# Eight groups of a graph layer's indirect row gathers put in other forms

## The chip, the cores and the metric

The kernel runs on one core of a Trainium2 chip. The metric is the device time of one execution in microseconds. The core has five engines with instruction streams of their own: PE (matrix multiply; its weight loads are shown apart as PEld), DVE and ACT (elementwise work), POOL and SP. SP, ACT and POOL can also issue DMA transfers; the gathers that this document is about, transfers whose source rows are named by a list of indices, are issued by POOL.

## The reference, cut to what matters

A graph layer over N = 12500 nodes with 256 values each and E = 200000 edges, sorted by their target node:

```python
h = jnp.maximum(_layernorm(x, axis=-1), 0.0)
agg = jax.ops.segment_sum(h[src], dst, num_segments=N)
z = (1.0 + eps_gin) * h + agg
t = jnp.dot(z, W1) + b1                       # 256 -> 512
t = jax.nn.relu(_batchnorm(t, g1, bt1))
conv_out = jnp.dot(t, W2) + b2                # 512 -> 256
out = x + jax.nn.relu(_batchnorm(conv_out + h, g2, bt2))
```

`h[src]` takes one row of 256 float32 values (1 KB) for every edge. All values of `src` lie between 0 and 12499.

## The kernel before, in words

The edges are cut into 1563 tiles of 128 (the last has 64), and the tiles into 131 groups of GT = 12 (line 19; the last group has 3). For each tile one indirect DMA on POOL (line 517) brings the 128 rows of its edges into SBUF, one row to a partition; its indices are a column of `srcT`, which holds all source numbers with the edge of a tile on the partition axis. The first LEAD = 30 groups (line 22) gather from `x` and normalise the rows afterwards (`settle`, line 376); the others gather from the DRAM table `h_tab`, into which the kernel has by then written the normalised rows (`h_chunk`, line 476).

The order is written out by hand (`manual_schedule`, line 367). The main loop (line 642) runs over the groups. In step i it calls `gather(i + AHEAD)` with AHEAD = 4 (line 21), then the additions, copies and comparisons that belong to earlier groups, and then `sums(i)` (line 556), in which PE multiplies the group's gathered rows by 12 selection matrices `oh` and adds them up in one PSUM tile (line 570). Between these products it places the sum of group i - 2 (`put`, line 583), turns chunks of h, and does a slice of the first dense product (`slice_of`, line 601). When the groups are done, the first batch norm is closed, and the second product (line 800), the second batch norm and the output follow; POOL has no part in that.

`gather(i)` (lines 509 to 521) chooses where the rows land by i % 5: remainders 0 and 1 use the fixed tiles gta0/gtb0 and gta1/gtb1 (8 and 4 rows to a partition, lines 123 to 127), the others a tile `gt` of a pool with three buffers. It goes through the group's tiles backwards. Tiles that `alone(i)` (line 462) names are left out: in every ninth group from 40 to 121 (40, 49, 58, ...) tile 0 is fetched row by row by SP and tile 1 by ACT (class `Fetcher`, line 398). These single rows are read as bytes, through views of both sides that are cast to U8, with an address that a register holds (lines 444 to 447).

Two lines of the gather:

```python
out=slot(ga, t - t0)[:rows], out_offset=None, in_=x if i < LEAD else h_tab,
in_offset=bass.IndirectOffsetOnAxis(ap=srcT[:rows, t : t + 1], axis=0),
```

Both sides are float32, and no bound is given.

Of the kernel before, what the change touches and what calls it, by code (L numbers as in the profile page):

```python
# [8 lines left out]
I32 = mybir.dt.int32  # L9
U8 = mybir.dt.uint8  # L10
# [7 lines left out]
EPS = 1e-5  # L18
GT = 12
MARGIN = 64  # L20
AHEAD = 4
LEAD = 30
EARLY = 2
# [17 lines left out]
def kernel(  # L41
# [17 lines left out]
    N, D = x.shape  # L59
# [9 lines left out]
    for g in range(NCH):  # L69
        rows = min(CH, N - g * CH)  # L70
# [11 lines left out]
    STEP = -(-N * P * GT // E)  # L82
    WIDE = P + 2 * MARGIN
    NBLK = -(-max(NTILE, NG * GT) // P)
# [4 lines left out]
    h_tab = dram.tile([N, D], F32, name="h_tab")  # L89
# [25 lines left out]
    srcT = consts.tile([P, NBLK * P], I32, name="srcT")  # L115
# [13 lines left out]
    def slots(ga, t, n=1):  # L129

        for lo, hi, tile_ in ga:
            if lo <= t < hi:
                assert t + n <= hi
                return tile_[:, t - lo : t - lo + n, :]

    def slot(ga, t):
        return slots(ga, t)[:, 0, :]
# [26 lines left out]
    with ExitStack() as es:  # L164
# [54 lines left out]
        place = raw.tile([P, NG], I32, name="place")  # L219
        nc.gpsimd.iota(place, pattern=[[STEP, NG]], base=-MARGIN, channel_multiplier=0)  # L220
        nc.gpsimd.iota(col_i, pattern=[[1, WIDE]], base=0, channel_multiplier=0)
        nc.gpsimd.iota(row_i, pattern=[[0, 1]], base=0, channel_multiplier=1)
        for i in range(EARLY):
            for t in reversed(range(GT)):
                nc.gpsimd.indirect_dma_start(
                    out=slot(early[i], t), out_offset=None, in_=x,
                    in_offset=bass.IndirectOffsetOnAxis(ap=srcE[:, i * GT + t : i * GT + t + 1], axis=0),
# [10 lines left out]
        ends = raw.tile([P, 2], F32, name="ends")  # L238
        for k, end in enumerate((P, 2 * MARGIN + 1)):
            nc.vector.memset(ends[:, k : k + 1], float(1 - end))  # L240
# [79 lines left out]
    def fast():  # L320
# [24 lines left out]
        with ExitStack() as fs:  # L345
# [8 lines left out]
            with ExitStack() as es:  # L354
                ln = es.enter_context(tc.tile_pool(name="ln", bufs=2))
                gat = es.enter_context(tc.tile_pool(name="gat", bufs=AHEAD + 1 - EARLY))
                sel = es.enter_context(tc.tile_pool(name="sel", bufs=2))
# [100 lines left out]
                sp, act = mybir.EngineType.SP, mybir.EngineType.Activation  # L458
                hf = Fetcher(nc.sync, sp, h_tab, SP_PACE, LEAD - AHEAD + 1, NG - 1, (0,), "s")
                af = Fetcher(nc.scalar, act, h_tab, ACT_PACE, LEAD - AHEAD + 1, NG - CLOSE, (1,), "a")  # L460

                def alone(i):
                    return {f.slots[0]: f for f in (hf, af) if i in f.groups}
# [3 lines left out]
                def x_chunk(g):  # L467
                    if g >= NCH:
                        return
                    n = chunks[g][1] * R  # L470
                    xts[g] = ln.tile([P, R, D], F32, name="xt", bufs=4)
                    if n < CH:
                        nc.vector.memset(xts[g], 0.0)
                    carry(nc.sync, xts[g], x, g, store=False)
# [34 lines left out]
                def gather(i):  # L509
                    t0, n = groups[i]  # L510
                    k = i % (AHEAD + 1)
                    ga = early[k] if k < EARLY else ((0, GT, gat.tile([P, GT, D], F32, name="gt")),)
                    for t in reversed(range(t0, t0 + n)):
                        if t - t0 in alone(i):
                            continue
                        rows = left if t == full_tiles else P
                        nc.gpsimd.indirect_dma_start(  # L517
                            out=slot(ga, t - t0)[:rows], out_offset=None, in_=x if i < LEAD else h_tab,
                            in_offset=bass.IndirectOffsetOnAxis(ap=srcT[:rows, t : t + 1], axis=0),
                        )  # L520
                    gathered[i] = ga

                def span(i):
                    return STEP * i - MARGIN, STEP * i - MARGIN + WIDE

# [96 lines left out]
                def first(c):  # L622

                    return min(i for i in range(NG) if c in reach(i))
# [4 lines left out]
                for g in range(3):  # L629
                    x_chunk(g)  # L630
                for i in range(EARLY, min(AHEAD, NG)):
                    gather(i)
# [3 lines left out]
                for c in range(NCH):  # L636
                    k = min(max(first(c) + 1, c + 2), NG - CLOSE - 1)
                    loads.setdefault(k, []).append(c)
                    scales.setdefault(min(max(first(c) + 3, c + 3), NG - CLOSE), []).append(c)
                    assert c + 1 < k <= first(c) + 4 and c < LEAD - AHEAD  # L640
                added = whole = 0
                for i in range(NG - CLOSE):
                    before = added
                    gather(i + AHEAD)
                    for k, f in enumerate((hf, af)):
                        if i == hf.begin - 8 + k:
# [53 lines left out]
                for i in range(NG - CLOSE, NG + 1):  # L700
                    if i + AHEAD < NG:
                        gather(i + AHEAD)
                    hf.step(i)
                    if i < NG:
                        spots(i)
                    if i + 1 < NG:
                        edges(i + 1)
                    for c in scales.get(i, ()):
                        z_scale(c)
                    while near < i:  # L710
                        hold(near)
                        while added < near - 1:
                            add(added)
                            added += 1
                        put(near)
                        near += 1
                    while added < near:
                        add(added)
                        added += 1
                    while whole < NCH and last(whole) < added:  # L720
                        queue += [(whole, f) for f in range(HC)]
                        whole += 1
                    for c, f in queue:
                        slice_of(c, f)
                        take(c, f)
                    queue = []
                    if i < NG:
                        sums(i)
# [363 lines left out]
```

## Time and profile before

| | us |
|---|---|
| median of 3 runs | 2174.43 |
| lowest and highest | 2173.98 and 2178.93 |
| the profiled execution's own time | 2174.26 |
| its span, first to last instruction | 2172.5 |
| POOL busy | 1463.4 (67%) |
| PE busy | 1604.0 (74%) |
| DVE busy | 802.1 (37%) |
| ACT busy | 408.9 (19%) |

The profile shows one execution. Its page has the busy time of each engine, a strip of the span in 40 slices (a digit is the busy share in tenths), the DMA queues, the chain of work that ended last, and the costliest groups of instructions: the line and the engine, what is written from what, how often, the busy time and the mean length in ns, the idle time of the engine just before, and what ended most of it. "issue" there means that the engine waited for nothing that the profile shows. Busy time on POOL counts the instructions that it works on and not the pieces between them. Other views give one line's instructions with their shortest, median and longest durations, an engine's instructions in order of time, and the busy time of all engines in a stretch.

In the chain that ended last POOL's lines have 33%, DMA 20%, PE 20% and issue 17%.

### The profile page before, as it was taken

To read this page: it belongs to the slowest core of one execution; us is meant where nothing else is said; L and a number is where in the kernel's file an instruction comes from. 1 tells how busy PE (TensorE), PEld (TensorE's weight loads), DVE (VectorE), ACT (ScalarE), POOL (GpSimd) and SP (SyncE) were. 2 spreads that over 40 slices of the span, in tenths; PEclk is the share of its full clock that TensorE was granted. 3 is DMA by queue.
4 is the path that set the end of the run, shared out by engine and by line. 5 is a ranking of instruction groups with operands and counts; after the bars stand their busy time and mean duration, and the time that the engine had idled before them with its cause. 6 is when DMAs were issued, how large, how long until landed. Compare 5 with 4: busy or idle time off the path is not lost.

```text
span 2172.5 us, 20945 instructions
## 1 busy us (share of the span) xinstructions
PE 1604.0 (74%) x4874; PEld 982.7 (45%) x4874; DVE 802.1 (37%) x1285; ACT 408.9 (19%) x772; POOL 1463.4 (67%) x1555
## 2 busy tenths in 40 slices
PE   4576667777777776777777777767777777779996
PEld 3454545554444444434444444434444444444445
DVE  5655657652323223223223222322322322323336
ACT  4666667520000000000000000000000000014446
POOL 7777777777777777777777777777777777750000
PEclk9877989888888889889888987888888888989998
DMA  6676777554444444444444444444444444547967
GB/s 197 211 228 215 252 234 233 171 148 123 131 128 136 116 128 135 123 123 134 122 130 129 120 129 130 135 117 127 137 121 121 136 119 123 154 129 269 307 232 286
DMA packets 153844, 349.86 MB, mean 161 GB/s; under 512 B 33564, under 2 KB 63916, under 8 KB 153710
## 3 DMA queue, kind: packets, MB, share of 16 engines
q0 software_dynamic: 74048, 202.28, 33.4%
q1 hardware_dynamic: 42534, 83.96, 11.7%
q10 hardware_dynamic: 37128, 62.19, 8.3%
q8 instruction: 41, 0.67, 0.1%
q14 instruction: 93, 0.76, 0.1%
HBM read 284.29 MB, written 64.00 MB: 160 GB/s over the span
## 4 chain that ended last, share of the span: by engine, by line
POOL 33%; DMA 20%; PE 20%; issue 17%; ACT 6%; DVE 3%; POOLq 0%; ACTq 0%; DVEq 0%
POOL gt L517 29%; PE ps L570 8%; PE py L800 8%; DMA gta<-h_tab,srcT 6%; DMA gtb<-h_tab,srcT 6%; DMA gt<-h_tab,srcT 5%; POOL gta L517 3%; DMA gt<-in_x_dram,srcT 2%; PE ph L606 2%; ACT gt L394 2%; PE pz L588 2%; ACT yT L825 2%; DVE stg L383 1%; ACT gta L394 1%; DMA gta<-in_x_dram,srcT 1%
## 5 line engine op out<-in xcount | busy, mean ns | idle before, releaser
L517 POOL DMA_INDIRECT gt<-h_tab,srcT x708 | 670.2, 947 | 215.8 <-issue 208.2
L570 PE MATMUL ps<-gt,oh 128*128 128x256 f32 x1848 | 613.0, 456 | 243.0 <-DMA gt<-h_tab,srcT 220.3
L570 PEld LDWEIGHTS ps<-gt,oh 128*128 128x128 f32 x1848 | 367.8, 220 | 488.7 <-DMA gt<-h_tab,srcT 337.3
L617 DVE BATCH_NORM_STATS2 st<-ph 128x6 f32<-128x512 f32 (+1 forms) x100 | 68.4, 684 | 949.6 <-PE ph L606 949.6
L517 POOL DMA_INDIRECT gta<-h_tab,srcT x315 | 297.8, 946 | 96.1 <-issue 42.1
L570 PE MATMUL ps<-gta,oh 128*128 128x256 f32 x822 | 264.0, 439 | 72.4 <-DMA gta<-h_tab,srcT 71.3
L619 ACT COPY ts<-ph 128x512 f32<-128x512 f32 (+1 forms) x26 | 14.1, 544 | 1434.8 <-DVE st L617 1434.8
L588 PE MATMUL pz<-at,zs 128*128 128x256 f32 x524 | 205.6, 534 | 87.1 <-ACT zs L577 78.5
L517 POOL DMA_INDIRECT gt<-in_x_dram,srcT x216 | 204.3, 946 | 65.8 <-issue 60.9
L570 PEld LDWEIGHTS ps<-gta,oh 128*128 128x128 f32 x822 | 158.9, 213 | 180.0 <-DMA gta<-h_tab,srcT 145.4
L570 PE MATMUL ps<-gtb,oh 128*128 128x256 f32 x416 | 158.9, 499 | 95.2 <-DMA gtb<-h_tab,srcT 69.6
L549 DVE TENSOR_TENSOR oh<-col,dstT 128x1536 f32<-128x1536 f32 x131 | 228.1, 1741 | 0.0
L606 PE MATMUL ph<-zc,w1s 128*128 128x512 f32 (+1 forms) x400 | 203.4, 637 | 29.7 <-DVE hc L503 28.6
L588 PEld LDWEIGHTS pz<-at,zs 128*128 128x128 f32 x524 | 141.4, 276 | 131.4 <-ACT zs L577 97.6
L517 POOL DMA_INDIRECT gtb<-h_tab,srcT x160 | 151.4, 946 | 48.7 <-PE ps L570 27.1
L800 PE MATMUL py<-ti,w2s 128*128 128x512 f32 (+1 forms) x400 | 170.8, 590 | 3.7 <-ACT ti L787 3.7
L570 PEld LDWEIGHTS ps<-gtb,oh 128*128 128x128 f32 x416 | 89.9, 239 | 147.6 <-DMA gtb<-h_tab,srcT 73.8
L599 DVE TENSOR_TENSOR zc<-pz,zc 128x512 f32<-128x512 f32 (+8 forms) x187 | 93.0, 522 | 121.5 <-PE pz L588 91.5
L606 PEld LDWEIGHTS ph<-zc,w1s 128*128 128x128 f32 x400 | 80.4, 205 | 95.9 <-issue 52.7
L800 PEld LDWEIGHTS py<-ti,w2s 128*128 128x128 f32 x400 | 76.9, 193 | 97.7 <-issue 90.1
L394 ACT ACTIVATE gt<-gt,nbg,rsg 128x256 f32<-128x256 f32 x216 | 108.1, 586 | 9.1 <-DVE nbg L392 7.6
L787 ACT ACTIVATE ti<-ti,of,sc 128x512 f32<-128x512 f32 (+1 forms) x100 | 76.4, 798 | 89.3 <-DMA ti<-t_tab 74.0
(111 smaller groups left out, 978.9 us busy)
## 6 DMA issues: line engine op xcount, KB each, us to landing
t_tab<-ts ACTq DMA_DIRECT2D x96, 256.0 KB
ti<-t_tab SPq DMA_DIRECT2D x96, 256.0 KB
one_s<-h_tab SPq DMA_DIRECT2D x1280, 1.0 KB
one_a<-h_tab ACTq DMA_DIRECT2D x1280, 1.0 KB
xt<-in_x_dram SPq DMA_DIRECT2D x24, 512.0 KB
h_tab<-ht ACTq DMA_DIRECT2D x24, 512.0 KB
h_cols<-hc SPq DMA_DIRECT2D x24, 512.0 KB
zc<-h_cols SPq DMA_DIRECT2D x24, 512.0 KB
```

What stands on the lines that cost most here:

```text
L383: nc.vector.bn_stats(st[:, c : c + 2, :].rearrange("p c s -> p (c s)"), two.rearrange("p c d -> p d c"),)
L394: nc.scalar.activation(slot(to, c), slot(v, c), AF.Relu, bias=nb[:, c : c + 1], scale=rs[:, c : c + 1])
L517: nc.gpsimd.indirect_dma_start(out=slot(ga, t - t0)[:rows], out_offset=None, in_=x if i < LEAD else h_tab, in_offset=bass.IndirectOffsetOn ...
L549: nc.vector.tensor_tensor(ohs[i][:, :n, :], col[:, :P].unsqueeze(1).to_broadcast([P, n, P]), dstT[:, t0 : t0 + n].unsqueeze(2).to_broadcas ...
L570: nc.tensor.matmul(ps, lhsT=oh[:rows, j, :], rhs=fetched[:rows], start=(j == order[0]), stop=(j == order[-1]))
L588: nc.tensor.matmul(pz[:, d, :], lhsT=zs[:, d * P : (d + 1) * P], rhs=at, start=True, stop=True)
L599: nc.vector.tensor_add(side, pz[:, :, a - lo : b - lo], side)
L606: nc.tensor.matmul(ph[:, :n], lhsT=w1s[:, d, f * P : (f + 1) * P], rhs=zc[c][:, d, :n], start=(d == 0), stop=(d == DC - 1),)
L617: nc.vector.bn_stats(st1[:, f, c, :], ph[:, :n])
L787: nc.scalar.activation(tis[g, f][:, :n], tis[g, f][:, :n], AF.Relu, bias=of1[:, f : f + 1], scale=sc1[:, f : f + 1],)
L800: nc.tensor.matmul(pys[d][:, :n], lhsT=w2s[:, f, d * P : (d + 1) * P], rhs=tis[g, f][:, :n], start=(f == 0), stop=(f == HC - 1),)
L825: nc.scalar.activation(yT[g][:, d, :], yT[g][:, d, :], AF.Relu, bias=of2[:, d : d + 1], scale=sc2[:, d : d + 1])
```

## The change

A table names eight groups and a form for each two of them; every other group is gathered as before. Groups 40 and 41 get a bound of N - 1 = 12499 with errors off, so that a row whose index were above it would be left out; groups 50 and 51 the same bound with errors on, the default; groups 60 and 61 view the landing tile and the table as int32; groups 80 and 81 view both as bytes, so that a row is 1024 elements. The list of indices, the rows that are read, their places, the order and the number of the gathers stay.

```diff
+FORMS = {40: "skip", 41: "skip", 50: "stop", 51: "stop", 60: I32, 61: I32, 80: U8, 81: U8}
...
                         rows = left if t == full_tiles else P
+                        to, table, more = slot(ga, t - t0)[:rows], x if i < LEAD else h_tab, {}
+                        if i in FORMS:
+                            kind = FORMS[i]
+                            if kind == "skip":
+                                more = dict(bounds_check=N - 1, oob_is_err=False)
+                            elif kind == "stop":
+                                more = dict(bounds_check=N - 1)
+                            else:
+                                to, table = to.bitcast(kind), table.bitcast(kind)
                         nc.gpsimd.indirect_dma_start(
-                            out=slot(ga, t - t0)[:rows], out_offset=None, in_=x if i < LEAD else h_tab,
-                            in_offset=bass.IndirectOffsetOnAxis(ap=srcT[:rows, t : t + 1], axis=0),
+                            out=to, out_offset=None, in_=table,
+                            in_offset=bass.IndirectOffsetOnAxis(ap=srcT[:rows, t : t + 1], axis=0), **more,
                         )
```

## The prediction

> **What bounds the kernel.** I read the strip of 40 slices first, then the costliest groups, then POOL's lines in order of time, and last the packet counts by queue. From the page:
>
> ```profile
> span 2172.5 us, 20945 instructions
> PE   4576667777777776777777777767777777779996
> POOL 7777777777777777777777777777777777750000
> L517 POOL DMA_INDIRECT gt<-h_tab,srcT x708 | 670.2, 947 | 215.8 <-issue 208.2
> L517 POOL DMA_INDIRECT gta<-h_tab,srcT x315 | 297.8, 946 | 96.1 <-issue 42.1
> L517 POOL DMA_INDIRECT gtb<-h_tab,srcT x160 | 151.4, 946 | 48.7 <-PE ps L570 27.1
> ```
>
> POOL's strip is flat at 7 from the first slice to the 35th. That looks like an engine with a quarter of its time free; it isn't. The group rows say why: 215.8 us of idle over 708 gathers is 0.305 us ahead of each one, and most of it ends in "issue", which means that nothing the profile shows was waited for. So one gather occupies POOL for 0.946 + 0.305 = 1.251 us and the next follows at once. The table of busy time by stretch gives the steady state:
>
> ```profile
> 457.00:1936.60 1479.60, 1097.04 (x3152) 652.41 (x3152) 422.27 (x630) 13.89 (x28) 1119.31 (x1183) 0.86 0.46 129
> ```
>
> The columns are the length, then busy time and count for PE, PEld, DVE, ACT and POOL, then clock, DMA share and GB/s. 1183 gathers in 1479.6 us are 1.251 us apiece: POOL alone accounts for the whole stretch. PE is busy 74% of it and DVE 29%, and in the list of waits POOL's own waits for another engine are all 0.3 us long, the same as the idle piece that it has ahead of every gather. POOL is never late for want of a free slot. So a change of d us in one gather of this stretch moves everything behind it by d, to the end.
>
> Are the gathers of the change in this stretch? Group 40's first gather starts at 607 us and group 81's last at about 1224 us (counting gathers in order along POOL's line), so all are. Groups whose number leaves 0 or 1 modulo 5 are those that land in gta0/gtb0 and gta1/gtb1, so each form will be visible under these names. Group 40 has two of its twelve tiles fetched by SP and ACT, the other seven have all twelve on POOL: 22 gathers "skip", 24 "stop", 24 as 32-bit integers, 24 as bytes, 94 in all. I make the sum against the profiled execution: 2174.26 us, of which the span is 2172.5; the median of the three runs is 2174.43, 0.17 higher. About 0.3% of it, 6.5 us, is what a measurement of this kernel can tell from no change.
>
> **What a row of a gather costs.** The last group gives the one gather with half the rows (64 instead of 128), the second line here, in POOL's order of time (start, duration, and in brackets the idle before):
>
> ```profile
> 1931.94 0.95 POOL L517 DMA_INDIRECT gt<-h_tab,srcT  x1 [0.30 <-issue]
> 1933.19 0.90 POOL L517 DMA_INDIRECT gta<-h_tab,srcT  x1 [0.30 <-PE ps L570]
> 1934.40 0.96 POOL L517 DMA_INDIRECT gta<-h_tab,srcT  x1 [0.30 <-PE ps L570]
> ```
>
> It took 903 ns beside 946 (shortest and median of the line's view), so 64 rows are worth 43 ns, one row 0.67 ns, and all 128 rows 86 ns. Over nine tenths of a gather is independent of its rows. This single gather is all that the trace has on the matter, and the chance below is set accordingly.
>
> **Part 1: the bound, 46 gathers (22 + 24).** No gather of before has one, so the price is bounded. What is added is a comparison of 128 indices with 12499; no index exceeds it, so nothing is ever skipped or reported, and "skip" and "stop" have one answer. The nearest row is the 0.67 ns: if comparing a row costs as much as all that is done for a row now, a gather grows by 86 ns, and 46 x 0.086 = 4.0 us. From below: the row part can't fall by more than itself, -4.0 us. From above: an instruction that goes over its indices in a second pass as long as its whole busy time, 0.946 us more, 46 x 0.946 = 43.5 us. Between ends so far apart I take 4.0, by the row that stands nearest, since the work is of the same kind (something done to every index) and the trace shows work per index to be cheap.
>
> [...]
>
> **Part 2: where the bound comes from.** A number of this kind may reach the instruction through a register, as the addresses of the single rows do on SP and ACT. The view of that line shows the price of setting one:
>
> ```profile
> L444 SPq MOVE one_s<-h_tab x1280: 29/29/38, 425.1 to 1590.0; - x183
> L444 SPq DMA_DIRECT2D one_s<-h_tab x1280: 227/228/402, 425.2 to 1590.1; - x183
> ```
>
> 29 ns (shortest, median, longest). I cost it at nothing: POOL's sequencer has 727 semaphore instructions of 17 ns among the gathers of this line, and the interval from one gather to the next has the median 1.251 us both where one lies in it (607 intervals) and where none does (935). They run under the gather ahead. With that cover gone it is 46 x 0.029 = 1.3 us.
>
> **Part 3: 32-bit integers, 24 gathers.** The same four bytes an element, both sides alike, the same 128 KB and the same number of rows in a gather. Nothing; bounds plus and minus the row part, 24 x 0.086 = 2.1 us.
>
> **Part 4: bytes, 24 gathers.** The row becomes 1024 elements of one byte. If POOL counts rows, nothing. If it counts elements, the row part is four times what it was, 3 x 86 = 258 ns, and 24 x 0.258 = 6.2 us. That a row stays whole on its way is likely from the single rows, which are read as bytes already. In the stretch from 1000 to 1300 us:
>
> ```profile
> q10 hardware_dynamic: 2736, 4.23, 4.0%
> one_a<-h_tab ACTq DMA_DIRECT2D x288, 1.0 KB
> t_tab<-ts ACTq DMA_DIRECT2D x15, 256.0 KB
> ```
>
> Columns of the first: packets, MB, share. 288 such rows at two packets leave 2160, which is 144 for each of the 15 stores (128 rows and 16 ends): a row of bytes is one packet and an end. I take nothing for this part.
>
> **What is late next:** nothing changes places. The landing of a gather (2.8 us, the median of the issue list) stays, SP's and ACT's rows are asked for by the order of the groups and their tiles are three deep, and PE, idle a quarter of the stretch, has room for four microseconds spread over 46 gathers.
>
> **Sum:** +4.0 + 0 + 0 + 0 = 4.0 us; 2174.26 + 4.0 = 2178.3 us.
>
> **Rivals.** (a) The bound is free, or the change does nothing that POOL notices: the comparison lies beside the work on the 0.86 us that doesn't depend on rows. Then 2174.3. For it: the rows are a tenth of the busy time. Against it: POOL works through its parts one after another, as the even intervals show. (b) The bound sends a gather through its indices one by one. Place: the 46 bounded gathers; price: up to a second busy time, 0.946 us, giving 2174.26 + 43.5 = 2217.8; it decides from 6.5/46 = 0.142 us a gather, 1.1 ns an index, which is less than twice what a row costs now. For it: that small margin, and that a list that may have holes could need other bookkeeping than a full one. Against it: the same list without bound costs 0.67 ns a row. [...] (c) Bytes are counted by the element: with part 1, 2174.26 + 4.0 + 6.2 = 2184.5. For it: that the element's kind is part of the instruction. Against it: the byte rows above. (d) Another form is shorter: the row part goes in all 94 gathers, 94 x 0.086 = 8.1 us, 2166.2. Only the lower bounds speak for it.
>
> **How the numbers follow.** Forecast 0.32 and (a) 0.24 both end within 0.3%: 0.56. (b) 0.30 and (c) 0.08 are slower: 0.38. (d) 0.06 is faster. The likeliest case's own range, from nothing gained to the register uncovered as well, is 2172 to 2180. The range I give reaches from 2170.2 (a bound that takes the row part away, -4.0) to 2217.8 (the second pass). [...]
>
> **What would show it.** The line's view, by gta and gtb in the windows of these groups, should have gathers of 1.03 us in 40, 41, 50 and 51, and of 0.946 in 60, 61, 80 and 81, with the idle of 0.30 unchanged. The software queue's packets now are 48 a gather and 32 for the half one (1542 x 48 + 32 = 74048, its row on the page) and should stay 74048; more would mean that bytes or skips cut rows up. PE, DVE and DMA rows should not move. I am wrong on part 1 if the bounded gathers take 1.09 us or more, on part 2 if the idle ahead of them is over 0.30, on parts 3 and 4 if 60 to 81 differ from 946 ns, and on the whole argument if these durations change and the end does not follow them.

## The result and the profile after

The changed kernel takes 2179.15 us (median of 18 runs, 2176.26 to 2184.23), the kernel before 2174.95 (18 runs beside them): 4.2 us more. The ratio is 1.0019 with the 95% interval 1.0012 to 1.0026, so the loss lies between 2.6 and 5.7 us. The forecast was 2178.3. The profiled execution is the fastest of the 18 (2176.26 us, span 2174.5).

The page after, the lines that answer to those shown of before:

```profile
span 2174.5 us, 20992 instructions
POOL 7777777777777777777777777777777777750000
q0 software_dynamic: 74048, 202.28, 33.5%
L527 POOL DMA_INDIRECT gt<-h_tab,srcT x708 | 670.7, 947 | 215.9 <-issue 209.5
L527 POOL DMA_INDIRECT gta<-h_tab,srcT x315 | 300.4, 954 | 96.1 <-issue 44.8
L527 POOL DMA_INDIRECT gtb<-h_tab,srcT x160 | 152.5, 953 | 48.8 <-PE ps L580 26.5
```

The tiles named gt, which no form touches, stay at 947 ns; gta and gtb, where the eight groups land, have risen from 946 to 954 and 953 on average, and the idle ahead of them has not moved (96.1 and 48.8 us, where it was 96.1 and 48.7). The packets are the same 74048. An average over 315 gathers hides who pays, so here is POOL in order of time (start, duration, idle before in brackets), inside one group of each form: 41 ("skip"), 50 ("stop"), 60 (integers), 80 (bytes), in four windows:

```profile
625.79 1.00 POOL L527 DMA_INDIRECT gta<-h_tab,srcT  x1 [0.30 <-PE ps L580]
627.10 1.00 POOL L527 DMA_INDIRECT gta<-h_tab,srcT  x1 [0.30 <-PE ps L580]
...
756.79 1.01 POOL L527 DMA_INDIRECT gtb<-h_tab,srcT  x1 [0.30 <-issue]
758.11 1.01 POOL L527 DMA_INDIRECT gtb<-h_tab,srcT  x1 [0.30 <-PE ps L580]
...
905.04 0.95 POOL L527 DMA_INDIRECT gtb<-h_tab,srcT  x1 [0.30 <-PE ps L580]
...
1201.84 0.95 POOL L527 DMA_INDIRECT gtb<-h_tab,srcT  x1 [0.30 <-PE ps L580]
```

In nanoseconds the medians are 999 in groups 40 and 41, 1012 in 50 and 51, 947, 947, 946 and 942 in 60, 61, 80 and 81, against 946 (942 in group 51) before. One gather now starts 1.30 or 1.32 us after the last instead of 1.25, and only in the bounded groups. The view of the gather's line shows what else came:

```profile
L527 POOLq MOVE  x46: 29/29/35, 599.1 to 777.8; - x46
```

These are 46 register writes on POOL's sequencer, one for each bounded gather. The first stands at 599.1 us, 8 us before the gather that it belongs to starts (607.5): the sequencer runs that far ahead. Following the start of each group in both traces, counted from the first gather, the kernel after is 0.28 us late at group 40, 1.46 at 42, 1.78 at 50, 3.75 at 52, 3.93 at 60, 3.90 at 62, 4.29 at 80 and 82, and 4.43 at POOL's end: two steps up, at the two bounded pairs, and none at the four groups of other kinds. Of the second step 0.32 us is one long gather (1328 ns in group 50). So the bound gives 22 x 0.053 + 24 x 0.066 = 2.75 us. Of the remaining 1.68 of POOL's lateness 0.15 are long gathers (those of before set off), 0.16 idle pieces, and 1.37 are about 1 ns on each of the gathers that nothing was done to (those from h_tab under 1 us have 945.4 ns on average before and 946.4 after). Two executions can differ by this much: the gathers from `x`, which no kernel here touches, have a median of 947 ns in the trace of the first experiment's first kernel and of 946 in that of its second.

The span does not show all of POOL's lateness. The stretch from POOL's end to the end of the span, before and after (length, then busy time and count for PE, PEld, DVE, ACT and POOL, then clock, DMA share and GB/s):

```profile
1936.60:2172.50 235.90, 210.95 (x630) 109.32 (x630) 103.89 (x150) 113.98 (x158) 0.01 (x1) 0.96 0.74 260
```

```profile
1941.10:2174.50 233.40, 209.53 (x631) 108.54 (x629) 103.79 (x150) 114.25 (x158) 0.03 (x1) 0.96 0.75 262
```

This last part, in which POOL has no work, happens to be 2.5 us shorter in the execution after, so that its span is only 2.0 us longer. The 4.2 us of the medians rest on 18 executions each; the pair of traces shows where POOL is late, and not the 4.2.

### The profile page after: what moved, and what is told of

It is laid out like the page before. It is cut to its first block, busy times and chain, and to the rows that moved or that the text cites. A ratio compares the mean times of both kernels' runs of the same rounds, so it can differ in the third digit from the quotient of the medians.

```text
span 2174.5 us, 20992 instructions
## 1 busy us (share of the span) xinstructions
PE 1597.2 (73%) x4874; PEld 974.6 (45%) x4874; DVE 802.0 (37%) x1285; ACT 409.1 (19%) x772; POOL 1467.7 (67%) x1555
## 3 DMA queue, kind: packets, MB, share of 16 engines
q0 software_dynamic: 74048, 202.28, 33.5%
## 4 chain that ended last, share of the span: by engine, by line
POOL 33%; DMA 20%; PE 19%; issue 17%; ACT 6%; DVE 4%; ACTq 0%; POOLq 0%; DVEq 0%; SPq 0%
POOL gt L527 29%; PE py L810 8%; PE ps L580 7%; DMA gta<-h_tab,srcT 6%; DMA gtb<-h_tab,srcT 6%; DMA gt<-h_tab,srcT 5%; POOL gta L527 3%; PE ph L616 2%; DMA gt<-in_x_dram,srcT 2%; ACT gt L395 2%; PE pz L598 2%; ACT yT L835 2%; DVE stg L384 1%; DMA gta<-in_x_dram,srcT 1%; ACT gta L395 1%
## 5 line engine op out<-in xcount | busy, mean ns | idle before, releaser
L527 POOL DMA_INDIRECT gta<-h_tab,srcT x315 | 300.4, 954 | 96.1 <-issue 44.8
L598 PE MATMUL pz<-at,zs 128*128 128x256 f32 x524 | 200.1, 522 | 90.2 <-ACT zs L587 83.1
L598 PEld LDWEIGHTS pz<-at,zs 128*128 128x128 f32 x524 | 136.3, 266 | 132.9 <-ACT zs L587 101.6
L527 POOL DMA_INDIRECT gtb<-h_tab,srcT x160 | 152.5, 953 | 48.8 <-PE ps L580 26.5
```

The source lines that it names most:

```text
L527: nc.gpsimd.indirect_dma_start(out=to, out_offset=None, in_=table, in_offset=bass.IndirectOffsetOnAxis(ap=srcT[:rows, t : t + 1], axis=0), ...
L598: nc.tensor.matmul(pz[:, d, :], lhsT=zs[:, d * P : (d + 1) * P], rhs=at, start=True, stop=True)
```

## The experiments

All but two put the 1183 gathers from h_tab (groups 30 to 130) into one form or two, so that a few ns a gather become tens of microseconds.

**The bound in every gather from h_tab, errors off and on.**

```diff
-FORMS = {40: "skip", 41: "skip", 50: "stop", 51: "stop", 60: I32, 61: I32, 80: U8, 81: U8}
+FORMS = {i: "skip" for i in range(30, 131)}     # the second kernel: "stop"
```

> All 101 groups that gather from h_tab (1183 gathers instead of 22) get the bound with errors off. Theory 1: the bound lengthens the gather itself by the 53 ns seen in groups 40 and 41 (999 beside 946), the MOVE ahead of it stays hidden, and POOL's pace sets the end: 1183 x 0.053 = 62.7 us, so about 2237 us, gathers of 0.999 us on gta, gtb and gt alike, idle ahead of them still 0.305. Rival 2: the 53 ns belong to the place (those two groups, or the tiles gta and gtb), and elsewhere a bound is free: then under 10 us. Rival 3: with a MOVE between all gathers the cover is no longer enough and the idle grows by 0.029 or more: 62.7 + 34 = 97 us, about 2271.

> The same 1183 gathers with the bound and errors on. Theory 1: 66 ns a gather as in groups 50 and 51 (1012 beside 946): 78 us, about 2252 us, some 15 us behind the form with errors off. Rival 2: errors on or off cost the same, and the 13 ns between the two pairs of groups came from their place: then the same time as with errors off, within 3 us.

Measured: 2590.5 us (ratio 1.0026, interval 0.9991 to 1.0061) and 2585.3 us (1.0034, 1.0002 to 1.0065), because on this chip the kernel before itself takes 2579.4. The gathers had the durations that theory 1 gave (medians 999 and 1012 ns, on gt as on gta and gtb, so rival 2 of the first is out: the price doesn't belong to a place). The median idle ahead of a gather is 0.305 us in both, with a MOVE for each, so rival 3's 0.029 us more is not there. But the end did not follow: of the second kernel's 78 us at most 17 arrived (0.65% of 2579). Why, is told below, where the microseconds are looked for.

**The same two, once more, on another chip.**

> The kernel with the bound, errors off, in all 1183 gathers from h_tab and a MOVE ahead of each, once more, in a job of its own. Theory 1 (the price is paid where POOL sets the pace, and the MOVE is hidden): if the kernel before takes about 2175 us here, 2175 + 1183 x 0.052 = 2236 us, as with the register written once (2239.5), and idle of 0.305 ahead of each gather. Rival 2 (the MOVE is paid on its own): 34 us more, 2270. If the kernel before takes some 2580 us here as well, POOL waits for others and the time is the same as before within 0.5%.

> The bound with errors on in all 1183 gathers once more. Theory 1 (errors on cost 13 ns more than errors off, once an instruction): where the kernel before takes about 2175 us, 2175 + 1183 x 0.066 = 2253 us, 15 to 16 us behind errors off in the same job. Rival 2 (errors on or off is no matter for the end): within 4 us of it.

Measured: 2571.6 us (1.0021, 0.9991 to 1.0050) and 2565.1 us (1.0018, 0.9990 to 1.0047), beside 2564.2 for the kernel before: again a chip on which POOL does not set the pace. The line's views (instructions, shortest, median and longest ns) of the first and of the second:

```profile
L527 POOL DMA_INDIRECT gt<-h_tab,srcT x708: 992/998/1332, 588.9 to 2287.8; - x177
```

```profile
L527 POOL DMA_INDIRECT gt<-h_tab,srcT x708: 1006/1012/1165, 582.2 to 2279.9; - x177
```

Errors on cost 14 ns more than errors off, at the same tiles. Whether this reaches the end, these two could not show.

**The bound in a register written once.**

```diff
-FORMS = {40: "skip", 41: "skip", 50: "stop", 51: "stop", 60: I32, 61: I32, 80: U8, 81: U8}
+FORMS = {i: "skip" for i in range(30, 131)}
...
+                pool = mybir.EngineType.Pool
+                bound = nc.alloc_register(pool, "bound")
+                nc.gpsimd.reg_mov(bound, N - 1)
...
-                                more = dict(bounds_check=N - 1, oob_is_err=False)
+                                more = dict(bounds_check=bound, oob_is_err=False)
```

> All 1183 gathers bounded with errors off, but the bound stands in one register that is written once instead of by a MOVE ahead of each gather. Theory 1 (the MOVE runs under the gather ahead of it and costs nothing): the same time as with a MOVE each, within 2 us. Rival 2 (the 53 ns are in part the MOVE's 29): 1183 x 0.029 = 34 us less than with a MOVE each.

Measured, on a chip on which the kernel before takes 2176.07 us: 2239.51, ratio 1.0295 (1.0270 to 1.0321), 63.4 us more; 1183 x 0.052 = 61.5. Lines of its page, of the gather's line, and of the stretch from group 30 to POOL's end:

```profile
span 2239.8 us, 20946 instructions
L530 POOL DMA_INDIRECT gt<-h_tab,srcT x708 | 710.9, 1004 | 216.0 <-issue 209.3
```

```profile
L530 POOL DMA_INDIRECT gt<-h_tab,srcT x708: 994/998/1481, 489.3 to 2000.5; - x177
```

```profile
458.00:2005.30 1547.30, 1117.75 (x3154) 640.93 (x3154) 421.74 (x630) 13.88 (x28) 1186.68 (x1183) 0.86 0.43 123
```

This is the run in which the whole argument can be checked, with the trace of before standing in for one on this chip: the stretch is 67.7 us longer than before's 1479.6, POOL's busy time in it 67.4 us more (1186.68 beside 1119.31), while PE's grows by 21 us and is 72% of the stretch, and DVE's doesn't grow. What POOL gains in length is the kernel's, one for one. The median gather here is 998 ns; the average is 1004 because 18 of the 1183 gathers were long (1.2 to 1.5 us, together 6.9 us over the median). There is no MOVE, and the gathers take what they take with one: in the two kernels below, run on this chip with a MOVE ahead of every bounded gather, they have the same 998 ns and the same 0.305 us of idle. Rival 2 is out. No kernel with a MOVE ahead of all 1183 gathers ran on a chip of this kind, so that theory 1's "same time" is shown by the durations and not by two times.

**Fewer rows, with and without bound.**

```diff
+PLACES = [i for i in range(32, 126) if i % 5 < 2 and i % 9 != 4]
+MIX = [(r, k) for r in (128, 96, 64, 32, 16) for k in (None, "skip", "stop")]
+FORMS = {i: MIX[n % len(MIX)] for n, i in enumerate(PLACES)}
...
+                            rows, kind = FORMS[i]
+                            to = to[:rows]
```

> In 37 groups the gathers bring only the first 128, 96, 64, 32 or 16 rows of each tile, without bound, with errors off, or with errors on, in turn; the other rows of those tiles are left out, so products of stale rows enter the sums and the output is not the reference's. Read from the gathers' own durations only. Without bound, by the prediction's 0.67 ns a row: 946, 925, 903, 882 and 871 ns for 128, 96, 64, 32 and 16 rows. Theory 1 (the bound is paid by the row, 53 ns / 128 = 0.41 ns): the difference to the unbounded gather of the same rows falls in proportion, 53, 40, 27, 13 and 7 ns. Rival 2 (paid once by the instruction): 53 ns at every number of rows. Errors on: 13 ns more at every number of rows if paid once, 13 falling to 2 if by the row.

Measured (33 groups, not 37; one run, 2173.47 us, where short gathers and bounds offset each other; medians of 24 or 36 gathers, ns):

| rows | no bound | errors off | errors on |
|---|---|---|---|
| 128 | 946 | 998 (+52) | 1012 (+66) |
| 96 | 916 | 964 (+48) | 977 (+61) |
| 64 | 908 | 947 (+39) | 960 (+52) |
| 32 | 872 | 915 (+43) | 928 (+56) |
| 16 | 847 | 890 (+43) | 903 (+56) |

Three rows of 16 in POOL's order of time, in three windows (none, errors off, errors on), show how the table was read:

```profile
1001.51 0.85 POOL L528 DMA_INDIRECT gta<-h_tab,srcT  x1 [0.31 <-issue]
...
1057.06 0.89 POOL L528 DMA_INDIRECT gta<-h_tab,srcT  x1 [0.32 <-PE ps L581]
...
1071.72 0.90 POOL L528 DMA_INDIRECT gta<-h_tab,srcT  x1 [0.30 <-issue]
```

An eighth of the rows, and the bound still costs 43 of its 52 ns: theory 1 (by the row) would have 7. From 16 rows to 128 at most 9 ns are added, 0.08 ns a row, so nearly all of the price is paid once by the instruction; errors on add 13 or 14 ns at every size. The rows themselves fall unevenly: 0.59 ns a row from 128 to 64, 0.88 on average from 128 to 16. With 16 rows I had expected 871 ns; it was 847.

**Bounds that leave rows out.**

```diff
+MIX = [None, 12500, 9375, 6250, 3125, 781]
+FORMS = {i: MIX[n % len(MIX)] for n, i in enumerate(PLACES)}     # PLACES as above
...
+                            more = dict(bounds_check=FORMS[i] - 1, oob_is_err=False)
```

> In 37 groups the bound, errors off, is none, 12499, 9374, 6249, 3124 or 780 in turn, so that none, none, a quarter, half, three quarters and some 94% of the rows are left out by the bound (stale rows take their places, so the output is not the reference's). Theory 1 (every index is compared, and a row that fails costs no less than one that passes): 999 ns for every bound, 946 without. Rival 2 (a row that is left out is work saved, 0.67 ns): 999 falling by up to 80 ns to about 920. Rival 3 (a list with holes goes another way): over 1.1 us as soon as a row is left out. The landing should come earlier and the packets be fewer in any case.

Measured (33 groups): medians of 998 ns for all five bounds and 946 without, idle 0.305. A gather that leaves out 94% of its rows costs POOL what one costs that leaves out none. In POOL's order of time, group 50, where the bound is 780, and the row of the software queue (packets, MB, share):

```profile
765.52 0.99 POOL L523 DMA_INDIRECT gta<-h_tab,srcT  x1 [0.30 <-DMA gta<-h_tab,srcT]
766.82 1.00 POOL L523 DMA_INDIRECT gta<-h_tab,srcT  x1 [0.30 <-DMA gta<-h_tab,srcT]
```

```profile
q0 software_dynamic: 74048, 182.75, 29.4%
```

The queue moved 202.28 - 182.75 = 19.53 MB fewer; by the bounds and evenly spread indices 12 x 128 x 1 KB x (6 x 0.25 + 5 x 0.5 + 5 x 0.75 + 5 x 0.94) is 19.6. So the rows are truly left out, and the packets are still 74048. I had expected fewer. The landing does come earlier, as expected: where the trace has it (7 to 10 gathers of each bound), its median is 2.81 us after the start without bound and with 12499, then 2.69, 2.61, 2.52 and 2.34.

This kernel also shows the bound, with a MOVE for each gather, reaching the end of POOL's work. Its one run took 2197.95 us beside 2176.07 for the kernel before, and this is the stretch from group 30 to POOL's end:

```profile
457.60:1957.00 1499.40, 1099.12 (x3152) 637.75 (x3152) 421.85 (x630) 13.88 (x28) 1138.88 (x1183) 0.87 0.40 114
```

It is 19.8 us longer than before's, with 19.6 us more of POOL's busy time: 324 x 0.052 = 16.8 for the bounded gathers, and most of the rest is long gathers.

**Integers and bytes in every gather from h_tab**, each alone, then both in turns (odd groups integers, even groups bytes), and that once more.

```diff
+FORMS = {i: I32 for i in range(30, 131)}                      # or U8
+FORMS = {i: I32 if i % 2 else U8 for i in range(30, 131)}     # in turns
```

> All gathers from h_tab see both sides as 32-bit integers. Theory 1: no change, within 0.1% of before (2 us), gathers of 0.946 us. Rival: the kind of number chooses another path on POOL whose price is under 2 ns a gather; with 1183 of them it would be up to 2.4 us either way.

> All gathers from h_tab see both sides as bytes, 1183 instead of 24. Theory 1: POOL counts rows, the time stays within 0.1% of before (2 us) and the gathers at 0.946 us; packets of the software queue stay 74048. Rival: something is paid by the element that 24 gathers could not show: from 2 ns a gather on it would be 2.4 us; by the prediction's rival (c), 0.258 us a gather, 305 us.

> All gathers from h_tab without bound, those of odd groups as 32-bit integers and those of even groups as bytes. Theory 1 (the kind of element is no matter to POOL): the ratio to before is 1 within its interval, gathers of 0.946 us in both, 74048 packets. Rival: a price under 2 ns a gather that few gathers could not show, up to 2.4 us either way; by the element for bytes (0.258 us), 150 us.

> The gathers from h_tab as integers (odd groups) and as bytes (even groups) once more, in a job of its own. The change measured 4.2 us more than before, and its 46 bounded gathers account for 22 x 0.052 + 24 x 0.066 = 2.7. Theory 1 (the 48 gathers in other kinds cost nothing and the rest of the 4.2 is within its interval): ratio 1 within its interval, gathers of 0.946 us. Rival (the missing 1.5 us are the 48 gathers', 0.031 us each, somewhere that their durations do not show, in their landing for one): 1183 x 0.031 = 37 us more, where POOL sets the pace, that is if the kernel before takes about 2175 us here.

Measured: ratios 0.9989 (0.9964 to 1.0014), 1.0009 (0.9981 to 1.0037), 1.0004 (0.9981 to 1.0028) and 1.0010 (0.9982 to 1.0038), beside 2579.4, 2579.4, 2564.2 and 2576.8 us for the kernel before. The views of the line in the first and the second:

```profile
L527 POOL DMA_INDIRECT gt<-h_tab,srcT x708: 940/946/1477, 586.8 to 2297.8; - x177
```

```profile
L527 POOL DMA_INDIRECT gt<-h_tab,srcT x708: 940/946/1422, 599.5 to 2303.9; - x177
```

The median is 946 in both, as without a form. The packets are 74048 in all four. All four ran on chips where POOL does not set the pace, so their times bear only on the rest of the kernel; that POOL pays nothing, these durations show, and the change's own trace above shows it where POOL sets the pace (no step at groups 60 and 80). That 1.5 us of the measured 4.2 come from the landing of the 48 gathers, the rival of the last run, was not put to the test on a chip where POOL sets the pace.

**Errors off without a bound.**

```diff
+                            if kind == "quiet":                   # in all groups from 30 on
+                                more = dict(oob_is_err=False)
```

> All 1183 gathers from h_tab without bound but with errors off, which the kernel before leaves on. Theory 1 (the 13 ns of errors on belong to the check of a bound): nothing changes, 0.946 us a gather, within 0.1% of before. Rival 2 (the 13 ns are paid by every gather that has errors on): 0.933 us a gather, 1183 x 0.013 = 15 us less than before, about 2160.

Measured: 2560.3 us, ratio 0.9995 (0.9963 to 1.0026), again beside 2564.2. The duration decides, and it needs no particular chip (the gathers from `x`, which no form touches, have medians of 946 and 947 ns here, and of 946 in the trace of before):

```profile
L529 POOL DMA_INDIRECT gt<-h_tab,srcT x708: 940/946/1319, 592.7 to 2281.4; - x177
```

It is 946, not 933: the 13 ns of errors on are paid only together with a bound, and without one there is nothing to be had by switching errors off. No experiment points to a version that is faster than the kernel before.

**Where the 62 microseconds went on the other chips.** The stretch from group 30 to POOL's end on the second of these chips, with integers and bytes in turns, then with the bound and errors off, then with errors on (columns as before; the fifth busy time is POOL's, then the clock that TensorE was granted):

```profile
548.90:2296.80 1747.90, 945.51 (x3097) 680.60 (x3096) 420.95 (x631) 19.08 (x40) 1121.92 (x1183) 0.73 0.37 108
```

```profile
549.70:2295.40 1745.70, 956.07 (x3092) 683.01 (x3090) 420.89 (x628) 18.93 (x40) 1182.46 (x1183) 0.73 0.37 108
```

```profile
543.10:2284.80 1741.70, 940.92 (x3108) 673.76 (x3109) 430.32 (x643) 22.27 (x47) 1197.05 (x1183) 0.73 0.37 109
```

POOL's busy time rises from 1122 to 1182 and 1197 us and the stretch does not grow. (The kernel with errors off and no bound has 1122.4 in a stretch of 1736.2 there, so single executions differ by 12 us; the 60 and 75 us are well beyond that.) With 1183 x 0.305 = 361 us of the idle that every gather has, 1747.9 - 1121.9 - 361 = 265 us are left in which POOL waits; with the bound, 202, and with errors on, 184. The longer gathers eat POOL's waiting. In the view of POOL's waits of the first of these kernels, some are far above 0.3 us:

```profile
POOL gta L527 <- remote: 105.1, 51, 9.9
...
POOL gt L527 <- PE ps L580: 80.4, 21, 7.9
```

("remote" is an end that the profile could not follow to its source; the columns are total us, times, longest.) PE, which frees POOL's slots, trails there: 21 of the waits for gt end in its products, 80.4 us together. From POOL's end to the end of the span the first of these kernels has

```profile
2296.80:2572.40 275.60, 249.74 (x770) 135.88 (x769) 118.23 (x172) 120.36 (x169) 0.00 (x0) 0.96 0.67 235
```

PE then has 770 products left, 630 in the same place before; 102 of them, instead of 10, belong to the sums of gathered rows, and they end 45 us after POOL, instead of 5. Why PE is slower there stays open. The granted clock is 0.73 against 0.86, but PE's busy time in the stretch is not longer (946 us beside 1097), and of the 164 us for which it is idle ahead of its products for gt 155 end in "issue", where the profile shows no wait; that the clock makes the stretch 18% longer was not shown.

## Why the prediction was right, and where it was not

**The bound on POOL's pace** holds where the prediction was made: intervals of 1.251 us, no wait but the 0.305, and the register kernel's stretch longer by POOL's added busy time, 67.7 beside 67.4 us. On the chips where POOL waits for others it does not hold: on the second of them POOL's busy time was 60 and 75 us longer, and the stretch did not grow.

**Part 1, the bound: the size was too large by half, the reason was wrong.** I took the comparison as work by the row and priced it at a whole row's worth, 86 ns a gather and 4.0 us. It costs 52 ns with errors off and 66 with errors on, 2.7 us in all, and it is not work by the row: 43 ns of it are there with 16 rows. The right order of size came from the bracket (nothing below, little above a row's worth) and not from the mechanism, and that 4.0 lies beside the measured 4.2 is luck: the bounded gathers account for 2.7. The 0.67 ns a row, read from one half gather, is 0.59 to 64 rows and 0.88 to 16 in the ladder, so that some 0.83 us of a gather, not 0.86, would be left without rows (an estimate, 847 less 16 x 0.88).

**"Skip and stop have one answer" was wrong**, by 14 ns a gather, with no index out of bounds in either; in this change 24 x 0.014 = 0.3 us.

**Part 2** was right: the bound does come through a register, 46 MOVEs of 29 ns, and they are free; gathers with a MOVE ahead and gathers without have the same 0.305 us between them.

**Parts 3 and 4** were right: medians of 942 to 947 ns, packets unchanged.

**The rivals.** (a), a free bound, is out by the gathers' own durations (999 and 1012 ns beside 946), and the ratio's interval leaves out 1. The even intervals that were held against it show one gather after the other (every 1.251 us), and nothing of what runs side by side within one. (b), an index at a time, is out: even the 66 ns are less than half of the 142 at which it begins to decide. With errors off the bound costs 52 ns in all, and from 16 rows to 128 it grows by 0.08 ns a row. (c) and (d) are out: no gather of bytes is longer, and no form is shorter. The ratio's interval lies within 0.3%, where 0.56 of the chance stood. The 2172 at which the likeliest case's own range begins comes out only with part 3's lower bound (2.1 us less); with nothing paid the sum is 2174.3.

**What stays open:** the measured 4.2 us against 2.7 that the bounded gathers account for. 2.7 lies inside the interval (2.6 to 5.7), at its end. In the trace the rest of POOL's lateness is long gathers, idle pieces and a nanosecond on all others, which differ between executions, but I have no run that repeats the bounded half of the change alone on a chip of this kind.

## What to carry to other kernels

Price a new form of an instruction per instruction as well as per element: bracket it by rows of the trace, then measure it with the form in all its places, where 52 ns become 62 us, and with the size varied, which tells the two apart. A gather's bound is cheap but not free (here 52 ns with errors off and 66 with errors on, on 946), and leaving rows out by it gives POOL no time back (998 ns with none of the rows left out and with 94% of them). And before a cost is added up along an engine, see on which chips that engine is the bound: here the same 62 us were the kernel's on one chip and did not reach the end on two others.

## What the runs showed of the hardware that I had not expected

A gather's POOL time hardly depends on what it moves: 847 ns for 16 rows, 946 for 128, 998 whether the bound leaves out none of the rows or 94% of them, with packets unchanged and bytes gone. The chip mattered more than any of the kernels: the kernel before takes 2175 us in the first comparison and 2176 on the chip of the register kernel, and 2564 to 2579 on three others, where its mean granted clock was 0.77 instead of 0.87 to 0.88. Each chip was used in one series of runs, so whether it is the chip itself was not shown. And single gathers of 1.1 to 1.5 us turn up in every trace, 1 in before's stretch and 18 in that of the register kernel, without anything that the profile shows ahead of them.
